# Layer 3's shared expert kept in a tile of its own for the last two quarters, and the first half's gathers in two quarters around the last spreading

## The chip, the core and the metric

The kernel runs on one core of a Trainium2 chip. The time is that of one execution on the device, in microseconds (us). Tensor work is done by TensorE (PE in the profile; PEld are its weight loads), element work by VectorE (DVE) and ScalarE (ACT). GpSimd (POOL) issues the indirect transfers, and SyncE (SP) the plain ones.

## The reference

The input is x, 4 rows of 1024 positions with 128 features. Four layers follow, each an attention-like mixing and a feed-forward part, each part of the form layernorm(x + f(x)). The change touches the end of layer 3, whose feed-forward part is a mixture of experts:

```python
p = softmax(x @ router_w.T + router_bias)     # 32 experts
w, idx = top_k(p, 4);  w = w / sum(w)         # the four likeliest, weights made to sum to one
routed = sum over the four of w * ((silu(x @ gate_w[e].T) * (x @ up_w[e].T)) @ down_w[e].T)
shared = (silu(x @ sgate_w.T) * (x @ sup_w.T)) @ sdown_w.T
x = layernorm(x + routed + shared)
```

An expert's hidden width is 128, that of the shared expert 512. The x of the last layernorm is the output.

## The kernel before, in words

The 4096 tokens lie as 32 tiles of 128 tokens. A quarter is 256 positions of all four rows, 8 tiles. For layer 3 there are three parts: a is quarters 0 and 1 (16 tiles), b is quarter 2 and c is quarter 3 (8 tiles each). x is one tile in SBUF, 32 x 128 values per partition, and xT its transpose.

For each part layer 3 does this:

- `l3_attn` (L1556): the norm, the projections with a SiLU (`u`, L1575), a Toeplitz mixing (L1632 to L1638), the output projection added to x (L1647), a second norm, the transposes into xT.
- `l3_route` (L1656): the logits, a softmax (L715 to L720), the four largest (L698 to L707), and then `positions` (L1239), which works out at which row of an expert list each token lands. It multiplies the mask on TensorE (`s<-mask`), goes on with some twenty steps on VectorE, and writes `pos` at L1280; the experts' numbers (`ids`, L1291) and the weights come after.
- `spread` (L1317): 4 indirect transfers per tile (L1305, in `indirect`) write x's rows to a list in HBM, `l3ra`, `l3rb` or `l3rc`. x must be what the layer's feed-forward part reads until they have been done.
- `l3_shared` (L1677): for each block of 4 tiles four `glu` (two products `pg` and `pu`, a SiLU at L743, a product `hs` at L744) and `down` into `py`. The result is added to x on VectorE at L1693. This add must come after the scatters of `spread`, which read x.
- `small_experts` (L1705): groups of four list tiles. A group is loaded (`xg`, which waits for all scatters of the part), transposed (`tp`, `xgT`), taken through its experts (`gu`, `sg`, `hg`, `hT`, `yp`), copied by ScalarE (`yg`, L1750) and stored to a list of results. The likely number of groups is fixed (20 for a, 12 for b and c); for what is beyond, there is an If (L1362, L1363).
- `collect` (L1385): 4 gathers per tile (`yt<-l3ya` and so on, L1305 again) into one of 8 buffers, and four weighted adds to x on VectorE (L1396). A ninth tile's gathers wait for the adds of the first. `finish` (L1788) norms a quarter and writes it out; for c, `close` (L1863) does gathers, adds, norm and output row by row.

So GpSimd issues 32 scatters for each 8 tiles of a part and later 32 gathers.

The order of the instructions is set by a planner in the program itself. Each piece of work is a generator that yields a cost in microseconds. `mix` (L241) takes a main generator and a side one, and lets the side one go on for as many units as the main one has yielded, times or divided by a pace. Each instruction of the side generator is put behind the latest main instruction of its engine, without a wait (`queued`, L231). `press` (L1850) runs the side generator alone until a name is on a list. `abreast` (L822 onward) takes several generators, the one with the smallest clock first. After an If the record of the latest main instructions is empty, so what is pressed there stands behind nothing.

At the end (L1928 to L1945), the side generator `on` holds: the attention and the routes of b; then, side by side, the spreading of b with the gathers of a on the one hand, and the attention and the routes of c on the other; then the spreading of c and the gathers of b. The main work is a's shared part and experts; then, after a press for b's spreading, b's shared part and experts; then, after a press for c's spreading, c's. `close` ends it.

Of the kernel before, what the change touches and what calls it, by code (L numbers as in the profile page):

```python
# [15 lines left out]
ALU = mybir.AluOpType  # L16
# [4 lines left out]
P = 128  # L21
B, L, D = 4, 1024, 128
# [7 lines left out]
TQ = L // NQT  # L30
QT = NT // NQT
# [11 lines left out]
E3, F3, K3 = 32, 128, 4  # L43
# [26 lines left out]
def tile_of(b, i):  # L70

    return i // 2 * QT + b * 2 + i % 2


class Kernel:
# [812 lines left out]
    def l2_attn(self, hf):  # L888
# [6 lines left out]
        with ExitStack() as low, ExitStack() as ctx:  # L895
# [114 lines left out]

            last = 4 * hf + 3
            d0, d1, d3 = (last - 3, 512), (last - 2, 384), (last, 128)
            full = [(j, 512) for j in range(4 * hf)]
            alone = lambda m: [[(m, *p) for p in ps] for ps in ([d0], [d1, d3])]
# [659 lines left out]
            yield from self.positions(cp, "l3" + part.name, mask, w, part.nt, E3, K3)  # L1674
            yield (10.0,)

    def l3_shared(self, part, sw):  # L1677

        nc, x = self.nc, self.x
        NC = FS3 // P  # L1680
        with ExitStack() as c2:
            hp = self.pool(c2, "l3sh" + part.name, 2)
            ps = self.pool(c2, "l3sp" + part.name, 2, space=PSUM)
            assert "l3" + part.name in self.listed
            wd = sw[:, 2, :].rearrange("p (c d) -> p c d", d=D)
            for blk in range(part.t0 // 4, (part.t0 + part.nt) // 4):
                h = self.tile(hp, [P, NC, BLK], "hs", bufs=1)
                for c in range(NC):
                    f = slice(c * P, (c + 1) * P)
                    self.glu(ps, hp, h[:, c, :], sw[:, 0, f], sw[:, 1, f], blk)  # L1690
                py = self.down(ps, h, wd, NC)
                s = slice(blk * 4, blk * 4 + 4)
                nc.vector.tensor_tensor(x[:, s, :], py, x[:, s, :], ALU.add)  # L1693
                yield (9.0,)

    def l3_wall(self, ctx, right=False):
# [88 lines left out]
    def l3_experts(self, part, wall):  # L1785
        return self.small_experts("l3", E3, part, wall)

    def finish(self, part):  # L1788

        for q in range(part.q0, part.q0 + part.nq):  # L1790
            self.norm(self.quarter(q))
            yield (5.0,)
            for b in range(B):
                t = tile_of(b, 2 * q)
                self.nc.sync.dma_start(
                    out=self.out[b, q * TQ : (q + 1) * TQ, :].rearrange("(k p) d -> p k d", p=P),
                    in_=self.x[:, t : t + 2, :],
                )
            yield (1.0,)

    def chain(self, *gens):
        for g in gens:
# [53 lines left out]
        yield from self.l2_route(part)  # L1856
        yield from self.spread("l2", part, K2)

    def last(self, part, yp):
        yield from self.collect("l3", part, K3, yp)  # L1860
        yield from self.finish(part)

    def close(self, part, yp):  # L1863

# [9 lines left out]
    def all(self):  # L1874
        a, rest = self.first, self.rest
        b, c = rest
        r = self.both[1]
        a2, m2, n2 = self.by_rows
        with ExitStack() as ctx:
            lgp = self.pool(ctx, "l2lg")  # L1880
            self.l2_lg = self.tile(lgp, [P, NT, E2], "lg")
            with ExitStack() as early:

                self.l0_setup(early)
                self.l2_wr = self.load(lgp, self.ins["l2_wr"])
                self.run(self.l0_attn((0, 1)))
                self.l1_setup()
                self.l2_setup()
                self.zero_lists("l1")
                self.run(self.l0_ffn((0, 1)))  # L1890
                self.run(self.l1_attn((0, 1)))

                self.run(self.l1_route(a))
                self.run(self.mix(self.l0_attn((2, 3), True), self.spread("l1", a, K1)))
                self.zero_lists("l2", "l3")
                with ExitStack() as c2:
                    wall = self.l1_wall(c2)
# [12 lines left out]
            on = self.served(  # L1910
                self.chain(self.rows_in(a2), self.onward(a, True)),
                (lambda: self.rows_done >= B + 2, self.routed(m2)),
                (lambda: self.rows_done == 2 * B, self.routed(n2)),
            )
            self.run(self.mix(self.l2_attn(1), on, drain=False))
            with ExitStack() as c3:
                with ExitStack() as c2:
                    wall = self.l2_wall(c2)
                    self.press(on, listed("l2m"))
                    self.run(self.mix(self.l2_experts(m2, wall), on, drain=False))  # L1920
                    self.press(on, lambda: {"l2n", "routed l3a"} <= self.listed)
                    sw, wall3 = self.l3_wall(c3, True)
                    on = self.chain(on, self.rows_in(m2))
                    self.run(self.mix(self.l2_experts(n2, wall), on, drain=False))
                self.press(on, listed("l3a"))
                yp = self.pool(c3, "l3y", 8)

                on = self.chain(  # L1928
                    on, self.collect("l2", n2, K2, yp, which=(0, 1, 4, 5)),
                    self.abreast(  # L1930
                        self.chain(self.l3_attn(b), self.l3_route(b)),
                        self.collect("l2", n2, K2, yp, which=(2, 3, 6, 7)),
                    ),
                    self.abreast(
                        self.chain(self.spread("l3", b, K3), self.when(listed("made l3a")), self.last(a, yp)),
                        self.chain(self.l3_attn(c), self.l3_route(c)),
                    ),
                    self.spread("l3", c, K3), self.when(listed("made l3b")), self.last(b, yp),
                )
                self.run(self.mix(self.chain(self.l3_shared(a, sw), self.l3_experts(a, wall3)), on, 0.75, False))  # L1940
                self.press(on, listed("l3b"))
                self.run(self.mix(self.chain(self.l3_shared(b, sw), self.l3_experts(b, wall3)), on, 0.75, False))
                self.press(on, listed("l3c"))
                self.run(self.mix(self.chain(self.l3_shared(c, sw), self.l3_experts(c, wall3)), on))
                self.run(self.close(c, yp))  # L1945
        bad = self.nc.values_load(self.flag[0:1, 0:1], min_val=0, max_val=1)
        with self.tc.If(bad > 0):
            with ExitStack() as ctx:
                lgp = self.pool(ctx, "l2lg2")
                self.l2_lg = self.tile(lgp, [P, NT, E2], "lg")  # L1950
                self.l2_wr = self.load(lgp, self.ins["l2_wr"])
                self.l2_attn_general()
                for p in self.by_rows:
                    self.run(self.routed(p))
                    with ExitStack() as c2:
                        self.run(self.l2_experts(p, self.l2_wall(c2)))
                    self.run(self.rows_in(p))
                for p in self.parts:
                    self.run(self.onward(p))
                    with ExitStack() as c2:  # L1960
                        sw, wall = self.l3_wall(c2)
                        self.run(self.l3_shared(p, sw), self.l3_experts(p, wall))
                        self.run(self.last(p, self.pool(c2, "l3y" + p.name, 5)))


@with_exitstack
# [162 lines left out]
```

## Time and profile before

| | |
|---|---|
| median of 4 runs | 2439.47 us |
| lowest and highest | 2434.96 and 2451.53 us |
| the profiled execution | 2440.15 us |
| its span in the profile | 2438.3 us |
| granted TensorE clock, mean | 0.822 |
| busy: PE, DVE, ACT, POOL | 66%, 52%, 33%, 32% of the span |

In the end of the kernel, of which the change speaks, these events carry the order of the work (us from the start of the span):

| event | time |
|---|---|
| first product of b's shared part | 2042.5 |
| `pos` of b is written (L1280) | 2049.9 |
| scatters of b, then the first 32 gathers of a | 2050.9 to 2133.4 |
| the other 32 gathers of a | 2162.4 to 2213 |
| `pos` of c is written | 2200.1 |
| scatters of c | 2214.3 to 2255.2 |
| gathers of b | 2272.7 to 2312.5 |
| the last add of c's shared part (L1693) | 2328.9 |
| c's experts, from the first transposes to the last copy | 2331.8 to 2380.5 |
| gathers of c | 2384.5 to 2424.2 |
| end | 2438.3 |

A row of the order of time reads: start, length, engine, line, operation, what is written and read, and in the bracket how long the engine was idle before and what ended that. "issue" is time in which the engine waited for nothing that the profile shows, and "remote" is an event that it cannot name. A row of the waits reads: engine, what it waited to do, whom for, us in total, times, the longest. A row by stretch gives for each engine the busy microseconds and, in brackets, the number of instructions.

### The profile page before, as it was taken

The numbers are of one execution on the slowest core, as the hardware profiler recorded it, in microseconds if no ns is written. First come the engines' busy times: TensorE is split into PE (matmuls) and PEld (weight loads), VectorE is DVE, ScalarE is ACT, GpSimd is POOL, SyncE is SP. The second block draws the span as 40 slices with busy tenths as digits, with TensorE's granted clock in tenths as the row PEclk, the third lists the DMA queues.
The fourth block names the chain that finished last, engine by engine and source line by source line (L and its number), as shares of the span: only waits on it lengthen the run. The fifth ranks groups of instructions, "written<-read, shape, count | busy, mean of one in ns | idle before, by whom it ended". The sixth has DMA issues, their size and how long they took to land. (4 is left out here: it accounts for less than half of the span.)

```text
span 2438.3 us, 27065 instructions
## 1 busy us (share of the span) xinstructions
PE 1608.3 (66%) x9017; PEld 956.6 (39%) x9017; DVE 1270.8 (52%) x3630; ACT 803.3 (33%) x1159; POOL 770.1 (32%) x701
## 2 busy tenths in 40 slices
PE   7535776975661775677968787877735798262480
PEld 3214333843330335544623232345424485151270
DVE  8767895655570564324545674564602275252352
ACT  5511372422330332212236564632201164040140
POOL 5531385145227002234132002002372102727404
PEclk9766788988785888789989998988977899586695
DMA  9930002334101014212130000031411141131232
GB/s 306 288 107 0 13 34 81 118 115 156 68 30 52 15 55 156 90 53 72 37 108 21 1 1 18 1 117 40 172 56 32 42 124 52 51 97 64 66 100 59
DMA packets 215530, 187.10 MB, mean 77 GB/s; under 512 B 16528, under 2 KB 194064, under 8 KB 214864
## 3 DMA queue, kind: packets, MB, share of 16 engines
q1 hardware_dynamic: 194672, 142.29, 18.4%
q0 software_dynamic: 20704, 42.86, 5.3%
q8 instruction: 84, 1.38, 0.2%
q14 instruction: 70, 0.57, 0.1%
HBM read 88.49 MB, written 96.60 MB: 76 GB/s over the span
## 5 line engine op out<-in xcount | busy, mean ns | idle before, releaser
L1059 ACT ACTIVATE pr<-sc 128x1024 f32<-128x1024 f32 x288 | 279.7, 1021 | 318.1 <-PE sc L157 183.6
L157 PE MATMUL gu<-ld,xgT 128*128 x640 | 168.9, 408 | 59.4 <-issue 31.3
L157 PE MATMUL sc<-qm,kT 32*128 32x512 f32 (+3 forms) x1536 | 197.4, 554 | 14.9 <-issue 9.2
L157 PE MATMUL s<-pr,va 128*32 128x512 f32 (+3 forms) x1536 | 176.6, 526 | 46.1 <-issue 26.2
L165 PE MATMUL tp<-ld,hg 128*128 128x128 f32 x624 | 100.9, 283 | 121.6 <-DVE hT L169 40.9
L157 PEld LDWEIGHTS gu<-ld,xgT 128*128 128x128 f32 x640 | 122.8, 203 | 86.1 <-issue 40.6
L157 PE MATMUL gu<-wall,xgT 128*128 x304 | 154.7, 635 | 2.7 <-ACT xgT L167 2.0
L169 DVE COPY hT<-tp 128x512 f32<-128x512 f32 x118 | 80.8, 685 | 132.9 <-PE tp L165 58.4
L165 PEld LDWEIGHTS tp<-ld,hg 128*128 128x128 f32 x624 | 79.2, 146 | 173.5 <-DVE hT L169 46.2
L1065 DVE TENSOR_TENSOR pr<-pr,ld 128x512 f32<-128x512 f32 (+1 forms) x160 | 92.1, 580 | 99.8 <-ACT pr L1059 96.7
L157 PEld LDWEIGHTS sc<-qm,kT 32*128 32x128 f32 x1536 | 84.5, 195 | 114.4 <-issue 78.0
L1736 DVE TENSOR_TENSOR hg<-sg,gu 128x256 f32<-128x256 f32 x160 | 65.5, 416 | 120.7 <-ACT sg L1735 104.7
L167 ACT COPY xgT<-tp 128x512 f32<-128x512 f32 x99 | 57.9, 586 | 196.7 <-PE tp L165 151.1
L1502 ACT ACTIVATE sg<-gu 128x512 f32<-128x512 f32 x76 | 45.1, 597 | 228.1 <-PE gu L157 110.7
L1305 POOL DMA_INDIRECT l1ra<-x,posl1a x64 | 94.8, 1481 | 60.7 <-DVE posl1a L1280 41.5
L1735 ACT ACTIVATE sg<-gu 128x256 f32<-128x256 f32 x160 | 60.7, 384 | 138.5 <-PE gu L157 74.7
L1305 POOL DMA_INDIRECT yt<-l1yr,posl1r x64 | 60.5, 946 | 140.2 <-DVE x L1396 79.0
L157 PEld LDWEIGHTS s<-pr,va 128*32 128x32 f32 x1536 | 38.7, 112 | 155.3 <-issue 109.0
L1504 DVE TENSOR_TENSOR hg<-sg,gu 128x512 f32<-128x512 f32 x76 | 51.7, 681 | 89.2 <-ACT sg L1502 84.8
L165 PE MATMUL tp<-ld,xg 128*128 128x128 f32 x396 | 66.2, 295 | 42.5 <-ACT hT L167 13.9
L1305 POOL DMA_INDIRECT l1rr<-x,posl1r x64 | 61.6, 963 | 99.4 <-DVE posl1r L1280 80.2
L1305 POOL DMA_INDIRECT yt<-l1ya,posl1a x64 | 69.6, 1088 | 69.8 <-DVE x L1396 29.6
(441 smaller groups left out, 3519.5 us busy)
## 6 DMA issues: line engine op xcount, KB each, us to landing
wall<-wall SPq DMA_DIRECT2D x16, 768.0 KB
l3ra<-zero SPq DMA_DIRECT2D x1, 6144.0 KB
ld<-in_l_w SPq DMA_DIRECT2D x2, 3072.0 KB
wall<-we SPq DMA_DIRECT2D x24, 256.0 KB
ld<-in_l_w SPq DMA_DIRECT2D x1, 6144.0 KB
l1ra<-zero SPq DMA_DIRECT2D x1, 5120.0 KB
l1rr<-zero SPq DMA_DIRECT2D x1, 5120.0 KB
xg<-l3ra SPq DMA_DIRECT2D x20, 256.0 KB
```

What stands on the lines that cost most here:

```text
L157: return self.nc.tensor.matmul(out, lhsT, rhs, start=start, stop=stop)
L165: nc.tensor.transpose(pt[:, k * P : (k + 1) * P], s, self.ident)
L167: nc.scalar.copy(dst, pt[:, : n * P])
L169: nc.vector.tensor_copy(dst, pt[:, : n * P])
L1059: nc.scalar.activation(pr, sc[h], AF.Exp)
L1065: nc.vector.tensor_tensor(d, d, cst["tril"].unsqueeze(1).unsqueeze(1).to_broadcast([P, 2, n, P]), ALU.mult)
L1305: ins = self.nc.gpsimd.indirect_dma_start(**kw)
L1502: nc.scalar.activation(sg, gu[:, 0, :], AF.Silu)
L1504: nc.vector.tensor_tensor(h, sg, gu[:, 1, :], ALU.mult)
L1735: nc.scalar.activation(sg, pg[:, :, 0, :], AF.Silu)
L1736: nc.vector.tensor_tensor(h[:, 2 * c : 2 * c + 2, :], sg, pg[:, :, 1, :], ALU.mult)
```

## The change

Two things are changed.

First, the shared parts of b and c no longer add to x. `l3_shared` gets a tile `sh` of 8 x 128 values per partition; ScalarE copies `py` into it, and after the part's experts one add on VectorE brings the whole tile to x. Since x is not touched, the shared part needs xT alone, and it now comes ahead of the routes' last step and of the spreading: the press ends at a new mark that `mark` sets when the attention is done ("mixed l3b", "mixed l3c"), the shared part is mixed with `on`, and only then the press goes on until the spreading is listed. The pace of c's experts is 0.75 instead of 1.0.

Second, the gathers of a are cut in two. Those of its first quarter (8 tiles, 32 gathers) stay behind the spreading of b; those of the second quarter come after the spreading of c, and before the gathers of b. `finish` takes one quarter.

The general branch at the end of the program, for another case of layer 2, calls the functions in their new form.

```diff
-    def l3_shared(self, part, sw):
+    def mark(self, name):
+        self.listed.add(name)
+        yield (0.0,)
+
+    def l3_shared(self, part, sw, sh=None):
...
                 py = self.down(ps, h, wd, NC)
-                s = slice(blk * 4, blk * 4 + 4)
-                nc.vector.tensor_tensor(x[:, s, :], py, x[:, s, :], ALU.add)
+                if sh is None:
+                    s = slice(blk * 4, blk * 4 + 4)
+                    nc.vector.tensor_tensor(x[:, s, :], py, x[:, s, :], ALU.add)
+                else:
+                    t = blk * 4 - part.t0
+                    nc.scalar.copy(sh[:, t : t + 4, :], py)
                 yield (9.0,)
...
-    def last(self, part, yp):
-        yield from self.collect("l3", part, K3, yp)
-        yield from self.finish(part)
+    def last(self, part, yp, q=0):
+
+        yield from self.collect("l3", part, K3, yp, q * QT, QT)
+        yield from self.finish(part.q0 + q)
...
                     self.abreast(
-                        self.chain(self.l3_attn(b), self.l3_route(b)),
+                        self.chain(self.l3_attn(b), self.mark("mixed l3b"), self.l3_route(b)),
                         self.collect("l2", n2, K2, yp, which=(2, 3, 6, 7)),
                     ),
                     self.abreast(
-                        self.chain(self.spread("l3", b, K3), self.when(listed("made l3a")), self.last(a, yp)),
-                        self.chain(self.l3_attn(c), self.l3_route(c)),
+                        self.chain(self.spread("l3", b, K3), self.when(listed("made l3a")), self.last(a, yp, 0)),
+                        self.chain(self.l3_attn(c), self.mark("mixed l3c"), self.l3_route(c)),
                     ),
-                    self.spread("l3", c, K3), self.when(listed("made l3b")), self.last(b, yp),
+                    self.spread("l3", c, K3), self.last(a, yp, 1), self.when(listed("made l3b")), self.last(b, yp),
                 )
...
-                self.press(on, listed("l3b"))
-                self.run(self.mix(self.chain(self.l3_shared(b, sw), self.l3_experts(b, wall3)), on, 0.75, False))
-                self.press(on, listed("l3c"))
-                self.run(self.mix(self.chain(self.l3_shared(c, sw), self.l3_experts(c, wall3)), on))
+                hold = self.pool(c3, "l3hold", 2)
+                for p in (b, c):
+                    self.press(on, listed("mixed l3" + p.name))
+                    sh = self.tile(hold, [P, QT, D], "sh")
+                    self.run(self.mix(self.l3_shared(p, sw, sh), on, 0.75, False))
+                    self.press(on, listed("l3" + p.name))
+                    self.run(self.mix(self.l3_experts(p, wall3), on, 0.75, p is c))
+                    s = slice(p.t0, p.t0 + QT)
+                    self.nc.vector.tensor_tensor(self.x[:, s, :], sh, self.x[:, s, :], ALU.add)
                 self.run(self.close(c, yp))
```

More of the change, by code (lines that the diff above doesn't have):

```diff
@@ L1683, in l3_shared @@
             ps = self.pool(c2, "l3sp" + part.name, 2, space=PSUM)
-            assert "l3" + part.name in self.listed
+            assert sh is not None or "l3" + part.name in self.listed
             wd = sw[:, 2, :].rearrange("p (c d) -> p c d", d=D)
@@ L1786, in l3_experts, with finish @@
         return self.small_experts("l3", E3, part, wall)
[L1788 to L1799, printed above, removed]
+    def finish(self, q):
+        self.norm(self.quarter(q))
+        yield (5.0,)
+        for b in range(B):
+            t = tile_of(b, 2 * q)
+            self.nc.sync.dma_start(
+                out=self.out[b, q * TQ : (q + 1) * TQ, :].rearrange("(k p) d -> p k d", p=P),
+                in_=self.x[:, t : t + 2, :],
+            )
+        yield (1.0,)
     def chain(self, *gens):
@@ L1962, in all @@
                         self.run(self.l3_shared(p, sw), self.l3_experts(p, wall))
-                        self.run(self.last(p, self.pool(c2, "l3y" + p.name, 5)))
+                        yp = self.pool(c2, "l3y" + p.name, 5)
+                        self.run(*(self.last(p, yp, q) for q in range(p.nq)))
 @with_exitstack
```

## The prediction

> **What bounds the kernel now.** I read the chain that ended last first: it ends in GpSimd's gathers (POOL yt L1305) of the last quarter, so I went to GpSimd's order of time from 2040 us on, then to who waited for whom in the same stretch, then to busy time by stretch, then to the DMA queues. All 192 row transfers of the tail (a: 64 gathers; b and c: 32 scatters and 32 gathers each) are issued by GpSimd, one per 1.25 to 1.27 us: 192 x 1.256 = 241 us of the 388 us from 2050.86 to the end. So the question is what GpSimd waits for. Its long waits stand in the bracket at the end of these rows (start, length, idle time before, releaser):
>
> ```profile
> 2050.86 0.99 POOL L1305 DMA_INDIRECT l3rb<-x,posl3b  x1 [148.20 <-ACT sg L743]
> ...
> 2162.36 0.95 POOL L1305 DMA_INDIRECT yt<-l3ya,posl3a  x1 [28.93 <-DVE x L1396]
> ...
> 2272.65 0.98 POOL L1305 DMA_INDIRECT yt<-l3yb,posl3b  x1 [17.40 <-DVE x L1396]
> ...
> 2384.54 0.94 POOL L1305 DMA_INDIRECT yt<-l3yc,posl3c  x1 [72.05 <-SPq L1363]
> ```
>
> The first (148 us) is for the routes of b, the second for the adds that free a gather buffer, the fourth, 72 us, for the experts of c. The waits of the other engines there (us in total, times, longest):
>
> ```profile
> DVE x L1693 <- remote: 75.6, 2, 40.7
> PE s L157 <- issue: 37.5, 17, 9.0
> DVE x L1693 <- DMA l3rb<-x,posl3b: 11.7, 1, 11.7
> ```
>
> L1693 is the add the change takes away. One of its waits, 11.7 us, is put to the scatter that reads x; the 40.7 us and 34.9 us are put to nothing the profile can name. Busy time by stretch tells why (columns: stretch, its length, then busy us and instructions of PE, weight loads, DVE, ACT, POOL, the clock, DMA share, GB/s):
>
> ```profile
> 2051.00:2063.00 12.00, 11.14 (x56) 6.85 (x54) 9.63 (x19) 3.40 (x6) 9.33 (x9) 1.00 0.24 79
> 2063.00:2141.00 78.00, 24.01 (x72) 15.16 (x70) 13.25 (x33) 6.04 (x10) 53.91 (x55) 0.62 0.15 47
> 2141.00:2162.00 21.00, 16.68 (x85) 14.18 (x86) 13.47 (x44) 8.01 (x17) 0.00 (x0) 0.77 0.34 96
> ...
> 2206.00:2260.00 54.00, 5.09 (x21) 3.97 (x21) 5.73 (x20) 1.94 (x4) 37.67 (x39) 0.59 0.15 53
> ...
> 2285.00:2318.00 33.00, 7.44 (x23) 3.04 (x21) 0.00 (x0) 0.60 (x1) 20.78 (x23) 0.59 0.16 46
> ...
> 2331.00:2380.00 49.00, 45.68 (x288) 40.63 (x288) 30.02 (x93) 25.32 (x51) 0.00 (x0) 0.97 0.42 125
> ```
>
> While GpSimd issues without a pause, the other engines work for some 12 us and then almost stop: 72 matmuls in 78 us, against 85 in the next 21 us and 288 in 49 us when GpSimd is silent. The same three times (2063, 2206, 2285), whatever the work is. The queue view of the first such stretch has one queue alone, that of the row transfers; that of 2331 to 2380 has the instruction queues too (packets, MB, share):
>
> ```profile
> q0 software_dynamic: 1792, 3.67, 14.6%
> ```
>
> ```profile
> q8 instruction: 3, 0.05, 0.5%
> q14 instruction: 1, 0.01, 0.0%
> ```
>
> I read this as: in a long run of row transfers the engines get no new instructions and stand until some 6 to 8 us after it ends (last gather issued 2132.5, DVE goes on at 2141.45; last 2311.5, then 2318.04). So most of L1693's 87 us is not L1693's; whatever stands there would stand.
>
> The Trainium skill, "Runtime: NRT & Kernel Launch", section "Instruction fetch mechanics", says that a sequencer refills its instructions by a DMA queue of its own and that crossing a block is "mostly hidden". No instruction packet in 78 us with 72 matmuls disagrees. By the rule the 40.7 us would be a true wait that the change removes and the sum below would fall to some 2405 us; I go by the rows.
>
> **The change, part by part.** The profiled execution took 2440.15 us, 1.85 us more than its span and 0.7 us above the median; I count in its span.
>
> 1. *Positions of b, later.* Now L1280 writes them at 2049.9, in the press ahead of the shared quarter. After, the first block of the shared quarter comes first and the position step (12 of the planner's units) is queued behind its instructions on TensorE and VectorE. That block's last matmuls end at 2052.5 to 2056.9 in the trace; from the position matmul (2039.86) to L1280 (2050.1) it is 10.2 us. So 2063 to 2067, say 2065: **+15 us** for GpSimd's restart, which nothing covers, since it has waited 148 us for just this.
> 2. *Hold.* Two adds of 0.69 us per quarter become two ACT copies of 128x512 from PSUM (0.59 us, as L1750) and one add of 128x1024 (2 x 0.58 to 0.69 us by L1065 and L1693): under 3 us of work for each quarter, beside the 40 us transfers for b; c's add is queued ahead of the closing adds, in part 6. The wait of 11.7 us goes with it, but it lies inside the run of transfers: next late is the instruction after it. The copy now waits for the same matmuls on ACT; behind it there stand the SiLUs of c's attention (u L1575, which waits 22.0 us in this stretch already) and the Toeplitz adds that wait for them. I give the removed wait back at 0 to 11.7 us, and take 0.
> 3. *Gathers of a, first half, before the spread of c.* 32 scatters of b and 32 gathers of a run as one stream, as now: 64 x 1.256 = 80.4 us, so 2066 to 2146.5; VectorE goes on 8 us later (as 2133.4 to 2141.45): 2154.5, **+13**.
> 4. *Positions of c.* Now at 2200.06, 58.6 us after VectorE's restart, with 8 of 13 expert steps of b done (8 hT copies by then). After, the position step stands behind the eleventh or twelfth: three or four more at 3.55 us (c's pace), 10.7 to 14.2 us, if they hide nowhere. 2154.5 + 58.6 + 12.5 = 2225.6. Bounds: none of the 12.5 (2213), or the adds of a's first half (32 x 0.34 = 11 us) on top (2237).
> 5. *Spread of c.* Now it waits for the second half of a's gathers (14 us from L1280 to 2214.3) and comes as one stream with part of them. After, it starts 1 us after L1280 and a's second half follows: 80.4 us, 2226.6 to 2307. c's experts need only the scatters (2267), but lie in the standstill: restart after 6.5 us, 2313.5. Now they start at 2331.8: **-18 us**. c's shared quarter, which now fills 2271 to 2329, lies before this; that is the gain of the whole change.
> 6. *Gathers of b, later.* Now they are done (2312.5) before c's experts; after, each needs a buffer that an add of a's second half frees, and the planner sets those behind c's sixth to eleventh expert step and one behind the If; behind them on GpSimd stand only c's gathers. On SP's queue the eight output transfers of a go out in two fours, in idle time. Experts of c: 49 us as now, plus 0 to 16 us where the gathers stop them; I take 6: 2368.5. If 4.5, the last buffer's gathers 5, landing 2.5, the first add 1.5: c's gathers start at 2382 (now 2384.5), 32 x 1.256 = 40.2, and 14 us from the last to the end as now: 2436. b's adds (11 us), two norms (8 us each) and the held add now stand on VectorE ahead of the closing adds: 0 to 20 us, since 40 us of transfers cover them only if VectorE is fed; I take 8: span 2444, **time 2446 us**.
>
> So c's gathers start 2.5 us earlier than now and the end comes 6 us later (2446 against 2440.15); this is within 0.5% of the time (2428 to 2452), which is about what a measurement of this kernel can tell from no change.
>
> **Rivals.**
>
> *Faster: the stall does not grow.* If c's attention and b's experts get their work into the first 12 to 20 us of each run, or into gaps at buffers, the positions of c come at about 2200 as now. 25.6 us less gives 2420; with b's tail hidden too, 2410. For it: in 2051 to 2063 all engines ran at full speed beside the transfers, and b's shared quarter will be done by then. Against it: 2063 to 2141 is too long for it, and b's experts wait for all 32 scatters (40 us), so they start inside the standstill. 0.25, at 2410 to 2427.
>
> *Slower: b's gathers catch c's experts.* In the last steps of c's experts GpSimd issues 28 to 32 gathers. If they run on without pause for more than some 12 us before the last group, its instructions and the If's come only 6.5 us after the run: 20 us of standstill (as 2285 to 2318, 33 us, less the 13 of good speed) in place of my 6, and the closing adds behind b's get the full 20 in place of 8: +18 to +26, 2464 to 2474. Decides from the point at which fewer than three of those steps are left when the run is 12 us old. For it: the third stretch above. Against it: the buffers come free one by one, which makes pauses. 0.22.
>
> *It doesn't do what it says.* If b's experts start no earlier and c's held quarter saves nothing, since both lie behind the same transfers, only the +15 us of part 1 is left: 2455. 0.08.
>
> **The numbers.** Forecast, 2446, 2430 to 2462 by the bounds of parts 4 and 6: 0.45, of it 0.32 within 0.5%, 0.11 slower, 0.02 faster. With the rivals: faster 0.27, same 0.32, slower 0.41. Range: 2412 to 2474, which leaves out a little of both rivals.
>
> **What would show it.** L1280 for b at 2063 to 2067 and the first scatter 1 us later; 64 transfers in one run to about 2147 with VectorE idle for tens of us within; L1280 for c at 2213 to 2237; c's transposes of xg starting 6 to 8 us after the last gather of a; b's gathers inside c's experts; the last 32 gathers from 2376 to 2392. It is wrong if engines work at full speed through a run of 64 transfers, if the positions of c come by 2205, or if c's experts take over 65 us.

## The result, and the profile after

The changed kernel takes 2449.72 us (median of 40 runs, 2439.98 to 2459.91); the kernel before, in 66 runs beside it, 2441.37. The ratio is **1.0032 [1.0022, 1.0042]**: slower by 0.3%, inside the half per cent that the forecast named. The profiled execution took 2442.66 us, its span is 2440.9; it lies 7 us below the median of its kernel, that of before 1 us below, so the profiles show 2.6 of the some 8 us between the medians. The mean granted clock hardly moved (0.819, before 0.822), nor did busy time (PE 1611.5 us, 66% again).

That so large a rearrangement moves the end by so little calls for an account. The path to the end can be cut into legs by seven events, all read from the order of time. The predicted column is the working above; it counts c's experts from their first transposes to their last copy, which on the same events are 2305.1 to 2379.6 here and 2331.8 to 2380.5 before.

| leg (us) | before | predicted | after |
|---|---|---|---|
| start of the span to the first scatter of b | 2050.9 | 2066.0 | 2055.4 |
| to `pos` of c (L1280) | 149.2 | 159.6 | 155.5 |
| to the first scatter of c | 14.2 | 1.0 | 1.0 |
| to c's experts (first load of `xg`) | 114.6 | 86.9 | 90.2 |
| c's experts, to their last store | 51.7 | 55.0 | **77.5** |
| to the first gather of c | 3.9 | 13.5 | 6.0 |
| to the end | 53.8 | 62.0 | 55.3 |
| sum: the span | 2438.3 | 2444 | 2440.9 |

Against before, the third and fourth legs gain 37.6 us and the fifth gives 25.8 of them back; the rest is 14.4 us of small delays: +2.6 in all.

GpSimd's order of time in the changed kernel answers to the rows shown of before (start, length, and in the bracket its idle time before and who ended it):

```profile
2055.37 1.22 POOL L1305 DMA_INDIRECT l3rb<-x,posl3b  x1 [155.82 <-issue]
...
2211.89 0.99 POOL L1305 DMA_INDIRECT l3rc<-x,posl3c  x1 [71.39 <-ACT sg L743]
...
2315.90 0.94 POOL L1305 DMA_INDIRECT yt<-l3yb,posl3b  x1 [23.75 <-DVE x L1396]
2338.32 0.94 POOL L1305 DMA_INDIRECT yt<-l3yb,posl3b  x1 [17.73 <-DVE x L1396]
...
2385.55 0.95 POOL L1305 DMA_INDIRECT yt<-l3yc,posl3c  x1 [6.06 <-DVE x L1396]
```

The 72.05 us that GpSimd stood before c's gathers are now 6.06. But the 71.39 before c's scatters are new, and 23.75 + 17.73 in b's gathers stand where 17.40 stood. It still has 192 transfers to issue, and its idle time has only moved to other places.

Who waited for whom in the tail, from 2040 us on (us in total, times, longest):

```profile
POOL yt L1305 <- DVE x L1396: 54.2, 5, 23.7
...
DVE x L1957 <- DMA l3rb<-x,posl3b: 30.5, 1, 30.5
...
PE tp L165 <- DMA xg<-l3rb: 26.3, 1, 26.3
...
DVE x L1957 <- ACT sh L1701: 12.7, 1, 12.7
```

L1957 is the new add that brings the held tile to x. The program has it behind the experts; the trace has it **ahead** of them: it waits 30.5 us for the scatters of b, longer than the 11.7 us that L1693 waited for them before. The wait that the change meant to take away has been moved and has grown. But beside it TensorE's transposes for b's experts wait 26.3 us for `xg`, whose load needs the same scatters. And by stretch (columns as in the prediction's table):

```profile
2068.00:2098.00 30.00, 6.57 (x10) 2.00 (x9) 0.06 (x1) 4.55 (x6) 22.87 (x24) 0.61 0.13 52
2098.00:2122.00 24.00, 13.57 (x36) 9.03 (x36) 9.67 (x24) 2.90 (x6) 19.02 (x16) 0.61 0.34 98
2122.00:2142.00 20.00, 0.00 (x0) 0.00 (x0) 0.55 (x2) 0.38 (x1) 14.15 (x15) 0.53 0.18 52
2142.00:2212.00 70.00, 55.42 (x322) 46.94 (x323) 49.03 (x188) 35.19 (x65) 0.11 (x1) 0.87 0.24 73
2212.00:2232.00 20.00, 13.54 (x56) 7.65 (x54) 7.28 (x20) 2.39 (x4) 15.35 (x16) 0.93 0.22 77
2232.00:2302.00 70.00, 12.88 (x38) 7.92 (x38) 4.54 (x9) 2.38 (x4) 45.60 (x48) 0.55 0.14 46
2302.00:2344.00 42.00, 37.25 (x224) 33.09 (x224) 20.43 (x53) 17.64 (x37) 8.24 (x9) 0.89 0.45 131
2344.00:2362.00 18.00, 5.23 (x25) 4.39 (x24) 2.00 (x8) 2.32 (x6) 10.97 (x12) 0.82 0.20 58
```

There are three standstills again: 2068 to 2142 beside the first 64 transfers, 2232 to 2302 beside the second 64, and a new one of 18 us inside c's experts, beside 12 of b's gathers. Between the first two 322 matmuls go through in 70 us.

### The profile page after: what moved, and what is told of

The parts are those of the page before. It is cut to its first block, busy times and chain, and to the rows that moved or that the text cites. A ratio compares the mean times of both kernels' runs of the same rounds, so it can differ in the third digit from the quotient of the medians.

```text
span 2440.9 us, 27041 instructions
## 1 busy us (share of the span) xinstructions
PE 1611.5 (66%) x9017; PEld 962.2 (39%) x9017; DVE 1275.4 (52%) x3628; ACT 803.6 (33%) x1161; POOL 772.3 (32%) x701
## 5 line engine op out<-in xcount | busy, mean ns | idle before, releaser
L157 PE MATMUL gu<-ld,xgT 128*128 x640 | 175.6, 420 | 67.8 <-issue 36.0
L157 PE MATMUL sc<-qm,kT 32*128 32x512 f32 (+3 forms) x1536 | 201.4, 562 | 20.6 <-issue 10.9
L165 PE MATMUL tp<-ld,xg 128*128 128x128 f32 x396 | 65.8, 294 | 67.8 <-DMA xg<-l3rb 26.3
L1504 DVE TENSOR_TENSOR hg<-sg,gu 128x512 f32<-128x512 f32 x76 | 51.7, 681 | 88.5 <-ACT sg L1502 46.9
L157 PE MATMUL pu<-xT,ld 128*128 128x512 f32 x104 | 62.8, 698 | 43.9 <-DVE hs L744 43.2
```

The source lines that it names most:

```text
L157: return self.nc.tensor.matmul(out, lhsT, rhs, start=start, stop=stop)
L165: nc.tensor.transpose(pt[:, k * P : (k + 1) * P], s, self.ident)
L1504: nc.vector.tensor_tensor(h, sg, gu[:, 1, :], ALU.mult)
```

## The experiments

The expectations name theories by letters. A is the prediction's account: in long runs of transfers the other engines nearly stop, and the change moves the work between such runs. B says that the gain is there, but the held add's new wait eats it. D says that the others stand for as long as the transfers run, with pauses or without, so that time added to the runs is added to the kernel. F holds the cut in a's gathers responsible. J came last: adds that nothing binds stand too early on VectorE. The other letters are explained where they occur.

One thing must be known to read the numbers. The first four experiments ran on a chip on which the kernel before takes 2430 us, near the 2441 us of the result above; the other eight ran on three chips on which it takes 2031 to 2037 us. Each ratio is to runs of the kernel before on the same chip, and only those are compared.

### On a chip like that of the result

**late_add**: the change, with both held adds put behind the experts' tenth step on VectorE.

```diff
+    def with_add(self, gen, p, sh):
...
+        for n, got in enumerate(gen):
+            if n == 10:
+                self.queued(add())
+            yield got
...
-                    self.run(self.mix(self.l3_experts(p, wall3), on, 0.75, p is c))
-                    s = slice(p.t0, p.t0 + QT)
-                    self.nc.vector.tensor_tensor(self.x[:, s, :], sh, self.x[:, s, :], ALU.add)
+                    self.run(self.mix(self.with_add(self.l3_experts(p, wall3), p, sh), on, 0.75, p is c))
```

> The change, with the two adds of the held tile put behind the tenth step of the part's experts on VectorE. In the changed kernel the add for b (L1957) stands on VectorE ahead of the Toeplitz mixing of c and waits 30.5 us for the scatters of b. Theory A (the engines get no new instructions in a long run of row transfers, so what stands at the wait matters little): VectorE wins only the 8 us or so until the standstill begins; 2441 to 2450 us. Rival B (the new wait is what eats the gain of the removed one): the positions of c come some 20 to 30 us earlier and the time falls to 2415 to 2430 us.

Measured: 2433.32 beside 2430.43, ratio 1.0017 [0.9997, 1.0037]. The 30.5 us wait is gone, and the time is what it was, as far as these intervals tell (the change: 1.0022 to 1.0042). B, which blamed this wait alone, falls. VectorE's order of time (start, length, and in the bracket the idle time before) says why:

```profile
2100.75 0.42 DVE L1744 TENSOR_TENSOR hg<-sg,gu 128x256 f32<-128x256 f32 x1 [29.87 <-issue]
...
2108.31 0.69 DVE L169 COPY hT<-tp 128x512 f32<-128x512 f32 x1 [2.70 <-remote]
2129.94 0.35 DVE L1396 SCALAR_TENSOR_TENSOR x<-yt,wkl3a,x 128x128 f32<-128x128 f32 x1 [20.94 <-DMA yt<-l3ya,posl3a]
```

VectorE now does the Toeplitz mixing that stood behind the held add, some 7 us, and then stands 29.87 us all the same: its next work is b's experts, and their transposes on TensorE wait 29.2 us in this trace for `xg`, that is for the same scatters of b. The first `hT` of b's experts is done 33.6 us sooner than in the change (2141.87), and then a weighted add for a stands in front of what follows and waits 20.94 us, until a's first 32 gathers end. I saw what this last row means only on the other chips, below.

**hold_only**: the held tile, but a's gathers in one piece ahead of c's spreading, as before.

```diff
-  self.chain(self.spread("l3", b, K3), self.when(listed("made l3a")), self.last(a, yp, 0)),
+  self.chain(self.spread("l3", b, K3), self.when(listed("made l3a")), self.last(a, yp, 0), self.last(a, yp, 1)),
...
-  self.spread("l3", c, K3), self.last(a, yp, 1), self.when(listed("made l3b")), self.last(b, yp),
+  self.spread("l3", c, K3), self.when(listed("made l3b")), self.last(b, yp),
```

> The change's first half alone: the shared parts held and early, the gathers of a in one piece ahead of the spread of c as before. Theory A: the second half of a's gathers trickles between b's experts again, so scatters of c and gathers of b make one run of 64 in place of scatters of c and gathers of a; c's experts start when that run ends, and b's gathers are out of the way of c's experts: gathers of c start some 15 to 25 us earlier, 2415 to 2435 us. Rival B (the new wait for the scatters at the held add decides): it is still there, so about the changed kernel's time, 2445 to 2455 us.

Measured: 2429.61, ratio 0.9994 [0.9974, 1.0013]. The gain that A allowed did not come; nor is it as slow as the change, as B had it.

**split_only**: the cut in a's gathers, with the shared parts as before (added to x at once, behind the spreading).

```diff
-                for p in (b, c):
...
+                self.press(on, listed("l3b"))
+                self.run(self.mix(self.chain(self.l3_shared(b, sw), self.l3_experts(b, wall3)), on, 0.75, False))
+                self.press(on, listed("l3c"))
+                self.run(self.mix(self.chain(self.l3_shared(c, sw), self.l3_experts(c, wall3)), on))
```

> The change's second half alone: a's gathers in two quarters around the spread of c, the shared parts added to x after the spread as before. Theory A: positions of b at 2050 and of c by 2205, 64 transfers to about 2287, then the rest of c's shared part (13 us) and c's experts (49 us) with b's gathers in them: gathers of c from 2370 to 2385, 2430 to 2450 us. Rival C (the split is what gains and the hold what loses): below 2425 us.

Measured: 2440.33, ratio 1.0037 [1.002, 1.0054]. C, by which the cut gains, falls. So here the hold (with the pace of c's experts, which goes with it) is worth nothing and the cut costs 0.4%; together (0.9994 x 1.0037 = 1.003) they make the 1.0032 of the change. Why the cut costs is not shown by this.

**pause**: the change, with two fills of a 128x1024 tile on GpSimd (some 2 us) after every four row transfers of the tail, scatters and gathers, 48 times: 96 us of added work in GpSimd's row, in order to break its runs up.

```diff
+    def pause(self, lay):
...
+        for _ in range(2):
+            ins = self.nc.gpsimd.memset(self.pad, 0.0)
...
+            self.pause(lay)
```

> The change, with two memsets of 128x1024 on GpSimd (about 2 us) after every four row transfers of layer 3's last parts, 48 times, so 96 us of GpSimd time more. Theory A (an unbroken run of row transfers keeps the others from their instructions): instruction packets appear within the runs, VectorE and TensorE go on through them, c's experts no longer start after the last gather of a but soon after the last scatter of c; the pauses cost GpSimd 96 us, of which the idle time it had in waits (71, 24, 18 and 6 us) can take up much: 2380 to 2460 us. Rival D (the others stand because of what the row transfers themselves occupy, whether there are pauses or not): the standstills last as long as the runs and the time rises by 60 to 95 us, 2505 to 2545 us.

Measured: 2450.73, ratio 1.0082 [1.005, 1.0115]. 96 us of added work lengthen the tail by 6.8 us (from the last store of a's experts to the end 417.3; in the change 410.5; one execution each, on two chips). D falls. Where the time came from is seen in the stretch of its trace with c's scatters, in which c's shared part lies (columns as above):

```profile
2221.00:2273.00 52.00, 19.92 (x94) 12.59 (x92) 11.92 (x29) 5.35 (x9) 43.22 (x45) 0.73 0.13 48
```

In the change these 94 matmuls are the 56 and 38 of the rows from 2212 and from 2232, and the last ends at 2295.2, 83 us after the first row's start, beside transfers without a gap. Here, with fills among the transfers, the last ends at 2241.1, 20 us after the stretch's start; for the rest of it the transposes of c's experts wait 37.4 us for `xg`, that is for c's scatters. c's experts load their first `xg` 2.4 us after the last scatter of c, in the change 51 us after it. So on this chip the unbroken run does slow the others, as A says. Instruction packets lie within its runs, as A forecast (two on q8 between 2118 and 2175, where there were 190 matmuls), but engines that work need them whatever slowed them before.

### On the other chips

**after_gaps1**, **after_gaps2** and **before_gaps2** were meant to find a profit in this: the change with one or two such fills after every four gathers of a and b (none at the scatters), and the kernel before with two. The diff is that of after_gaps1; the others have `range(2)`.

```diff
...
+        if lay != "l3" or self.pad is None or part.name not in ("a", "b"):
+            return
+        for _ in range(1):
+            ins = self.nc.gpsimd.memset(self.pad, 0.0)
...
```

> The change, with one memset of 128x1024 (0.95 us) on GpSimd after every four gathers of a and b, 24 times (23 us); the scatters and c's gathers run unbroken as before. In the run with a pause after every four transfers of all kinds, the engines still stood beside the scatters, where TensorE waits at tp for xg, but went at full speed beside the gathers. Theory A (beside gathers the engines lack instructions, and a gap lets them through): b's experts work on beside a's gathers, the positions of c come 15 to 40 us earlier than at 2211, c's experts start soon after c's last scatter; 2375 to 2420 us. Rival D2 (one microsecond is too short a gap, and what helped was 2 us): 2450 to 2475 us, the gaps are only lost.

> As the run before, with two memsets (about 2 us) after every four gathers of a and b, 46 us in all. Theory A: the gaps are long enough, 2385 to 2425 us, a little slower than with one memset if one is enough. Rival D: 2465 to 2500 us.

> The kernel before, with two memsets (about 2 us) after every four gathers of a and b. Theory A: the same standstills beside the gathers go (2093 to 2141 and 2285 to 2318), but the scatters of c still come after all gathers of a, now with 32 us of gaps in front of them, and the add of the shared part still waits for the scatters: 2395 to 2440 us, and slower than the change with the same gaps by 10 to 30 us, since then the change's early scatters of c and early shared part count. Rival E (the change brings nothing even with engines that are fed): within 5 us of the change with the same gaps.

Measured: 2100.83, 2115.27 and 2075.81 beside 2037.19; ratios 1.0306 [1.0263, 1.0348], 1.0377 [1.0334, 1.0419] and 1.0196 [1.0153, 1.024]. The profit did not come, and against expectation the change with the same gaps is 39 us slower than the kernel before with them. This chip is 400 us faster with the same kernel, and it has no standstill of this kind to break. One and the same stretch, the scatters of layer 1's part r, before (first) and in the run after_again (second, on another chip of this kind), whose programs differ in nothing there:

```profile
725.00:795.00 70.00, 9.94 (x33) 3.00 (x26) 2.10 (x7) 1.02 (x1) 50.94 (x54) 0.52 0.13 51
```

```profile
711.00:781.00 70.00, 59.12 (x537) 28.96 (x534) 46.30 (x110) 33.05 (x35) 51.96 (x51) 0.95 0.19 73
```

GpSimd does the same in both (54 and 51 transfers). Beside it TensorE does 33 matmuls on the one chip and 537 on the other.

**after_again** is the change itself, with no edit, beside the kernel before on such a chip; **after_gaps1_again** repeats after_gaps1 there.

> The change itself, once more beside the kernel before, because in the last call the kernel before took 2037 us on its chip in place of 2441 us. If this chip is like the first one (before at 2430 to 2445 us), theory A and all others expect 1.000 to 1.006 of before. If it is like the other one (before at about 2037 us), theory F says that the engines go at full speed beside the transfers there, that GpSimd's transfers are the bound, and that the split puts 32 gathers (40 us) from GpSimd's idle time to behind c's scatters: 1.010 to 1.025 of before; rival G says that the change loses only through standstills, and so gains where there are none: 0.975 to 0.995.

> The change with one memset of 128x1024 (0.95 us) on GpSimd after every four gathers of a and b (23 us in all), as in the run of that name, beside the kernel before on this chip. On a chip like the first one, theory A: c's experts work beside a's gathers, 0.975 to 0.992 of before; rival D2 (one microsecond is too short): 1.008 to 1.020. On a chip like the other one: 1.025 to 1.035, as there.

Measured: 2105.19 and 2100.88 beside 2036.1, ratios 1.034 [1.0314, 1.0365] and 1.0333 [1.0305, 1.0362]. The change costs some nine times as much here: 69 us, more than F said (1.025 at most), and G, which forecast a gain, falls. The gaps neither cost nor bring anything. VectorE's order of time shows two waits where nothing but a transfer was late:

```profile
1806.02 1.23 DVE L1957 TENSOR_TENSOR x<-sh,x 128x1024 f32<-128x1024 f32 x1 [30.48 <-DMA l3rb<-x,posl3b]
...
1817.56 0.69 DVE L169 COPY hT<-tp 128x512 f32<-128x512 f32 x1
1846.74 0.35 DVE L1396 SCALAR_TENSOR_TENSOR x<-yt,wkl3a,x 128x128 f32<-128x128 f32 x1 [28.50 <-DMA yt<-l3ya,posl3a]
```

The first is the held add again, beside which TensorE waits 26.1 us for b's `xg`. The second is the first weighted add of the **last gathered tile** of a's first quarter. It stands right behind the first `hT` of b's experts and waits there for the end of all 32 gathers. The next `hT` is behind it, and with it TensorE and ScalarE. These adds are pressed into the program after the If of b's experts, where the record of latest instructions is empty, so nothing binds them to a place, and, as I read it, they were set where VectorE seemed free. That is J. The standstill it makes (columns as above):

```profile
1825.00:1847.00 22.00, 0.00 (x0) 0.00 (x0) 0.26 (x1) 0.00 (x0) 16.51 (x19) 0.57 0.25 68
```

**no_a0**: the change without the 32 gathers and 32 adds of a's first quarter. It leaves out the routed part of the output of that quarter.

```diff
-  self.chain(self.spread("l3", b, K3), self.when(listed("made l3a")), self.last(a, yp, 0)),
+  self.chain(self.spread("l3", b, K3), self.when(listed("made l3a")), self.finish(a.q0)),
```

> The change without the 32 gathers and 32 adds of a's first quarter, which leaves the routed experts' output of that quarter out. It takes the run of transfers away that lies beside b's experts. Theory A (the run of gathers stops the other engines): with b's scatters done 45 us after the restart, b's experts and the rest of c's attention go at full speed from there, and the positions of c come 35 to 45 us earlier than in the change on a chip like the first one: 0.982 to 0.988 of before. Rival H (b's experts and c's routes are slow by themselves, by the order of their instructions): the positions of c come less than 15 us earlier, 0.996 to 1.004 of before.

Measured: 2048.77, ratio 1.0068 [1.0045, 1.0091]. 56 us less than the change beside it. The 28.5 us wait is gone (the one at L1957 is still there, 27.75), b's experts store their last result at 1872.1 instead of 1904.9, and `pos` of c comes at 1875.5 instead of 1909.9, 34 us earlier, so H (less than 15) falls. This kernel has 40 us less of transfers, so it does not tell how much is the wait's.

**adds_bound** comes nearer: everything of the change, but the held adds and the adds of the last gathered tiles, with what the side generator yields until then, are queued behind the experts' last step, ahead of the If (`flag` is "added a0" for b and "added a1" for c, and `last` sets it when its adds are listed).

```diff
...
+            if n == 12:
+                self.queued(add())
+                while flag not in self.listed:
+                    self.now += self.queued(on)[0]
...
```

> The change, with the held adds and the adds of the last gathered tile of a's two quarters put behind the experts' last step ahead of the If. In the change they come after an If, where the planner's record is empty, so nothing holds them back, and they stand on VectorE ahead of the experts: it waits there 30.5 us for b's scatters, 28.5 us for the last gathers of a's first quarter (in the run after_again), 23.4 us for c's scatters, and TensorE and ScalarE wait behind it. Theory J (these adds are the standstill beside the gathers): b's experts go on through a's gathers; the positions of c come 20 to 45 us earlier after b's scatters than in the change (115 us on the first kind of chip, 106 us on the other); on a chip like the first one 0.985 to 0.998 of before, on one like the other 1.000 to 1.018 (the change: 1.003 and 1.034). Theory A (the row transfers themselves stop the engines): less than 8 us of change, 1.000 to 1.004 and 1.030 to 1.035.

Measured: 2058.96 beside 2030.52, ratio 1.0129 [1.0108, 1.0149]. Of 3.4% it takes away 2.1, some 41 us (on two chips of this kind), **by the place of instructions alone**, a few adds above all; transfers and work are the same. The stretch that answers to the empty 22 us, beside the same gathers (columns as above):

```profile
1828.00:1848.00 20.00, 20.00 (x149) 18.86 (x147) 16.14 (x50) 10.19 (x20) 15.12 (x17) 1.00 0.63 175
```

149 matmuls beside a's gathers, at a granted clock of 1.00. `pos` of c comes 78 us after b's last scatter starts, in the change 106, and c's experts take 50.0 us from their first load to their last store, in after_again 79.3. J holds. It is the last tiles' adds, more than the held ones: VectorE still stands 29.3 us in front of b's experts, whose transposes wait 28.6 us for b's scatters; gone are the 28.5 us behind the first `hT` and a like wait of 25.0 us, for the end of a's other gathers, in c's experts. Each was not tried alone. What is left of the loss is in GpSimd's order of time, in its only two waits of over 10 us in the tail:

```profile
1764.19 1.22 POOL L1305 DMA_INDIRECT l3rb<-x,posl3b  x1 [113.84 <-issue]
...
1886.01 0.99 POOL L1305 DMA_INDIRECT l3rc<-x,posl3c  x1 [37.43 <-issue]
```

From 1886.01 on it issues transfer after transfer, with no wait over 0.31 us, to the last at 2047.9. So it is the start of b's scatters (25.1 us after a's last store; 12.1 in before_gaps2, which has the old order) and the 37.4 us until c's positions are there, that make the tail. No trace of the unchanged kernel was taken on such a chip to set beside them.

**hold_bound**: the same binding, with a's gathers in one piece, as in hold_only. The diff is against adds_bound, beside that of hold_only.

```diff
-                    flag = "added a0" if p is b else "added a1"
+                    flag = "added a1"
```

> The same binding of the adds, and a's gathers not split (all ahead of the scatters of c): what is left of the change is the held tile and the early shared part. Theory J with F (the split moves 40 us of GpSimd's work behind c's scatters, where GpSimd is the bound): 0.975 to 0.995 of before on a chip like the first one, 0.995 to 1.010 on one like the other, and below the run beside it by 5 to 25 us. If the split is harmless once the adds are bound: the two runs within 5 us of each other.

Measured: 2096.97, ratio 1.0322 [1.03, 1.0343]. The expectation failed, and the waits of the trace say why (us in total, times, longest):

```profile
DVE x L1396 <- DMA yt<-l3yb,posl3b: 61.6, 8, 56.4
...
PE py L157 <- DVE hs L744: 58.6, 3, 55.6
```

Here the adds for b's last two tiles are the ones that nothing binds. The first stands in c's shared part, and TensorE waits 55.6 us for the `hs` behind it. So the kernel differs from adds_bound by such a wait as well as by the cut, and F can't be judged from it. None of the kernels of this section is faster than the one before beyond its interval. adds_bound was not run on a chip like that of the result.

## Why the prediction came out right

The number was right (2446 predicted, 2449.72 measured, ratio within half a per cent as forecast), but as the sum of errors that cancel, and so in part by luck. Leg by leg, measured less predicted: -10.6, -4.1, 0, +3.3, +22.5, -7.5, -6.7, together -3.1.

**Part 1, positions of b: right in size.** +15 was predicted; measured from a's last store to L1280 it is 24.0 us, before 11.2: +12.8. On the clock they came only 4.5 us later, since a's experts ended 8.3 us earlier in this execution; this is most of the -10.6. Whether it is the change's stays open: from `pos` of a to that store it is 297.0 us here and 304.7 before, 297.5 and 297.1 in late_add and hold_only, 303.0 in split_only, which has no held tile, but 303.6 in pause, which has it; on the other chips 218.5 in after_again and 219.9 in before_gaps2.

**Part 2, the hold: its sum held, its picture did not.** It said that the removed wait of 11.7 us lies inside the run of transfers and brings nothing. It missed that the held add itself would be placed ahead of b's experts and wait 30.5 us. late_add shows that on this chip taking that one wait away moves the time by no more than the intervals allow: b's experts, which come next, wait for the same scatters, and a wait of 20.94 us for a's gathers then shows behind it.

**Part 3, the run of 64: its length right, its reason in doubt.** 80.4 us were predicted, and from the first scatter of b to the last of a's first 32 gathers it is 84.2. VectorE took up `hT` at 2141.87, 2.3 us after the last gather was issued, not 8; ScalarE went on at 2146.1 and TensorE at 2147.3, 6.6 and 7.8 us after it. "The engines get no new instructions" is not shown. From 2056 to 2150 the trace has no instruction packet at all, and yet the engines went on from 2141.9 to 2147.3; had they stood for lack of instructions, I would expect it to end with a packet. What is seen, beside the wait for b's scatters, is a slow pace. Eight products of `gu` on this chip (first fence; TensorE, start, length, idle time before), and the same step in after_again:

```profile
2109.64 2.02 PE L157 MATMUL gu<-ld,xgT 128*128 x4 [3.25 <-issue]
2115.35 2.08 PE L157 MATMUL gu<-ld,xgT 128*128 x4 [3.69 <-DVE hg L1744]
```

```profile
1820.24 1.89 PE L157 MATMUL gu<-ld,xgT 128*128 x8
```

7.8 us against 1.9, with waits that the profile puts to nothing or to an element step that is late itself. The queues of the stretch with 33 and 537 matmuls, again first before, then after_again (packets, MB, share):

```profile
q8 instruction: 1, 0.02, 0.1%
```

```profile
q8 instruction: 4, 0.07, 0.5%
q14 instruction: 2, 0.02, 0.1%
```

The Trainium skill, "Runtime: NRT & Kernel Launch", section "Instruction fetch mechanics", says that instructions come in blocks of 256. The 537 matmuls and 534 weight loads with four packets on q8 agree with that, if q8 is TensorE's queue, which the trace does not say. By it, as an estimate, the 72 matmuls and 70 weight loads of the prediction's stretch need a packet at most once. So their row does not disagree with that section, as the prediction had it, and no run here shows whether a crossing is "mostly hidden": the absence of packets, on which the prediction built, is what a slow pace of any cause would leave.

That the unbroken run is a cause of it on this chip is shown by pause (the 94 matmuls in 20 us in place of 83). By what way it slows the others, and why on some chips only, stays open. The slow pace also hides J's second wait in the changed kernel on this chip: the first `hT` was itself not done before 2141.87, when the gathers had ended, and three adds behind it follow without a wait. On the other chips `hT` was done 29 us before them. With the first wait gone, in late_add, the second shows here too. What both together cost on this chip was not tried, so how much of its standstill from 2068 to 2142 is the slow pace, how much J and how much the plain wait for b's scatters is open.

**Part 4, positions of c: right.** 155.5 us after the first scatter (predicted 159.6, bounds 147 to 171), behind b's experts, and 69.0 us after VectorE went on (predicted 71.1). The last store of b's experts was at 2206.1.

**Part 5, spread of c at once: right, and its gain is there.** One stream of 80.3 us (predicted 80.4), c's experts 27 us earlier than before. The reason was not quite the one given. They waited for c's shared part, and only at the end perhaps for the run, as SyncE's own waits between 2200 and 2306 say for the load of `xg` (L1336):

```profile
SPq L1336 <- DVE hs L744: 36.6, 1, 36.6
...
SPq L1336 <- remote: 12.0, 1, 12.0
SPq L1336 <- DMA l3rc<-x,posl3c: 4.8, 1, 4.8
```

The shared part's four last `hs` came at 2255.8, 2266.3, 2277.5 and 2289.4, 10 to 12 us apart, in the slow pace. The load came at 2302.14, together with ScalarE's copy of `py`; this last wait, 12.0 us, the profile cannot name. It ends 10.9 us after the last gather of a was issued and 7.0 us after the shared part's last product, so it can belong to either.

**Part 6, c's experts: the mis-sized term.** 49 us plus 6 for b's gathers were predicted; measured are 77.5, or 74.5 on the events that the prediction counted. Its own sign of being wrong, over 65 us, came true. This is the mechanism of the slower rival, "b's gathers catch c's experts": 25 matmuls in the 18 us from 2344 to 2362, then 40 in 24 (2362 to 2386). I had put it at 20 us in the rival, and took 6 in the sum; it came in full. What I had set beside it did not come: the 13.5 us from the experts to c's gathers were 6.0, and the 8 us of b's adds in the close were 1.5 (55.3 against 53.8). So the rival was right in its mechanism and wrong in its sum, and the forecast the other way round. On the other chips c's experts take as long, 79.3 us, for another reason, J's wait of 25.0 us; in adds_bound, without it, they take 50.0. "The stall does not grow" did not happen on this chip, and "it doesn't do what it says" neither, since c's experts did start earlier.

Of the other signs that it named, the first scatter 1 us after L1280, the unbroken run of 64, b's gathers inside c's experts and c's gathers at 2385.6 came; L1280 for b (2054.4) and for c (2210.9) came earlier than named, and c's transposes started 13.9 us after the last gather of a, not 6 to 8. Two of its sums do not add up: the slower rival's +26 gives 2472, not 2474, and all bounds of parts 4 and 6 together give some 2420 to 2479, wider than the 2430 to 2462 that it took.

## What to carry to other kernels

An instruction that this planner's record of order does not bind can be set ahead of work that does not need it, so what waits for the last transfer of a long run must be bound behind the work that it should not hold up; here the place of a few adds was worth some 41 us on the chips where it was tried. But ask first whether the work behind a wait could have run: taking the held add's wait of 30.5 us away brought no gain that the intervals show, since the experts behind it waited for the same transfers. When one engine issues all the transfers, count its idle time and not the waits that a change removes: here 72 us before c's gathers turned into 71 before c's scatters. And judge a change only beside runs of the old kernel on the same chip, and on several chips if possible: this one was worth +0.3% and +3.4%.

## What the runs showed of the hardware

One and the same program took 2441 and 2430 us here and 2031 to 2037 there, a sixth less. No chip of the experiments was measured at a second time, so the runs do not separate the chip from the moment. The mean granted clock differs by less (0.82 and 0.87 to 0.88). What the traces show to differ is the pace of the engines beside long runs of GpSimd's row transfers: 33 matmuls on one chip and 537 on another in the same 70 us. Pauses of 2 us after every four transfers helped the pace on the first; on the others, after every four gathers, pauses of 1 us changed nothing and pauses of 2 us cost time (1.0377 against 1.0306). The row transfers themselves take the same on both: 0.94 to 0.96 us each, one per 1.25 to 1.27 us.
